# Latent attention's output divided by its sums between two 32 by 32 transpositions on VectorE, and the range test on ScalarE

## The chip, the cores and the metric

The kernel runs on one core of a Trainium2 chip. The core has five engines, each with a queue of its own: TensorE (PE in the profile; PEld is its loading of weights), VectorE (DVE), ScalarE (ACT), GpSimd (POOL) and SyncE (SP, which here only issues DMAs). TensorE writes its results to PSUM, which has eight banks of 512 float32 columns in 128 partitions. The metric is the time of one execution on the device in microseconds (us), the median of three runs.

## The reference

The input is x, 8 sequences of 1024 tokens with 256 features. Two blocks follow one another, each with a residual: x = x + attention(layernorm(x)), then x = x + local(layernorm(x)). The change concerns the first, a latent attention with 16 heads of 16 features and a rotary part of 32 that all heads share:

```python
c_kv = x @ W_kv_down
k_rope = _rotary_apply(c_kv @ W_k_rope, cos, sin)
k = (c_kv @ W_k_up).reshape(Bb, Tt, NH, HD)
v = (c_kv @ W_v_up).reshape(Bb, Tt, NH, HD)
q = (x @ W_q).reshape(Bb, Tt, NH, HD)
q_rope = _rotary_apply(x @ W_q_rope, cos, sin)
scores = jnp.einsum('bqhd,bkhd->bhqk', q, k)
scores = scores + jnp.einsum('bqr,bkr->bqk', q_rope, k_rope)[:, None]
scores = scores / scale
scores = jnp.where(causal[None, None], -jnp.inf, scores)
w = jax.nn.softmax(scores, axis=-1)
attn = jnp.einsum('bhqk,bkhd->bqhd', w, v).reshape(Bb, Tt, D_MODEL)
return attn @ W_o
```

The second block, two layers of windowed attention and a gated feed-forward part, takes the larger share of the time and isn't touched.

## The kernel before

The latent attention takes the eight sequences ("batches") one after the other, in 36 steps each. A step is one unit of scores: for one half c of the queries (512 columns), one group g of four heads and one block kb of 128 keys, TensorE computes four score blocks (sc, L422), transposed, with keys in the partitions. ScalarE takes their exponential (pt, L430). VectorE multiplies it by er (L444), the exponential of the shared rotary scores, which is computed once for all heads. TensorE then multiplies by the values (acc, L455). The values have a column of ones beside the 16 of each head, so acc holds, in 32 partitions for each head, 16 rows of output, one row of sums in row 16, and rows that nothing uses.

The work is staggered by steps. In step s TensorE's queue has the scores of unit s and then acc of unit s-2; VectorE's has the products of unit s-1. PSUM gives two pairs of banks to the scores, two banks to acc, and two banks in turn ("bank") to everything else. Everything else is put beside the steps by a table written by hand ("beside", with a step, a batch relative to the present one, a method and its arguments): the residual of the batch before, and the normalisation, projections and rotary scores of the next one or two. The methods are called in that order, and the order of the calls is the order of each engine's queue, for this part of the program. The local layers have an order of their own.

What the change touches:

- rotary (L395 to L406) computes one block of the shared rotary scores in a bank, psR. ScalarE writes er, the exponential, and with it the row sums (most). VectorE takes the row minima of er (least). GpSimd then cuts the triangle of the block on the diagonal. At the end of the stage most and least are compared with bounds (L609, L610): where exponentials are out of range, a flag makes a general version of the kernel run after this one.
- value (L369 to L382) computes the values of two token blocks, and VectorE copies them from PSUM (L76 in the helper).
- When acc of a group is complete, ScalarE copies it to SBUF (oaT). One step later, finished (L467 to L475) lets TensorE transpose it in four pieces of 128 by 128 (pst, L203), so that tokens lie in the partitions; VectorE takes the reciprocals of the sums (rs, L472) and multiplies (onat, L473).
- out_turn (L478 to L488) transposes two token blocks of onat back on TensorE (pso), and ScalarE copies them (oT). out_add (L490 to L501) multiplies by W_o (psx), VectorE adds x (L500), and a DMA stores the result.
- verdict (L1652 to L1657) tests rs for its range, three small VectorE instructions.
- In the last batch, out_turn and out_add of its first half are held back to the end ("held"), and only the attention itself is left after step 15.

Of the kernel before, what the change touches and what calls it, by code (L numbers as in the profile page):

```python
# [81 lines left out]
def preln_mla_local_kernel(  # L82
# [72 lines left out]
    def mla(ctx: ExitStack, verdict):  # L155
# [46 lines left out]
        def flip(out, t):  # L202
            nc.tensor.transpose(out, t, ident)  # L203
# [13 lines left out]
        nc.sync.dma_start(wknat, W_k_up)  # L217
        wv = wp.tile([P, D], F32, name="wv")
        nc.sync.dma_start(wv, W_v_up)
        wout = late.tile([P, 2, D], F32, name="wout")  # L220
        nc.sync.dma_start(wout, W_o.rearrange("(c p) d -> p c d", p=P))

# [42 lines left out]
        class Batch:  # L265
# [129 lines left out]
            def rotary(self, c, kb):  # L395
                q0, w, er = self.block(c, kb)
                ps = bank(f"psR{self.b}_{c}_{kb}")
                times(ps[:, :w], self.rk[:, kb * P : (kb + 1) * P], self.rq[:, q0 : q0 + w], True, True)
                n = 12 * self.b + 8 * (1 - c) + kb
                nc.scalar.activation(er, ps[:, :w], AF.Exp, scale=SCALE, accum_out=most[:, n : n + 1])  # L400
                nc.vector.tensor_reduce(least[:, n : n + 1], er, AX.X, ALU.min)  # L401
                if q0 == kb * P:
                    nc.gpsimd.affine_select(  # L403
                        out=er[:, :P], in_=er[:, :P], pattern=[[1, P]],
                        compare_op=ALU.is_ge, fill=0.0, base=0, channel_multiplier=-1,
                    )  # L406

            def start(self):
                b = self.b
                self.onat = late.tile([P, NT, NH, HD], F32, tag="onat", name=f"onat{b}")  # L410
                self.rs = small.tile([P, NT, NH], F32, tag="rs", name=f"rs{b}")
                self.acc = {}

            def scores(self, key, parts):

# [49 lines left out]
                return ended  # L465

            def finished(self, c, g, oT):  # L467
                ps = bank(f"pst{self.b}_{c}_{g}").rearrange("p (i h d) -> p i h d", i=4, h=4)
                for i in range(4):
                    flip(ps[:, i].rearrange("p h d -> p (h d)"), oT[:, i * P : (i + 1) * P])  # L470
                r = self.rs[:, 4 * c : 4 * c + 4, 4 * g : 4 * g + 4]
                nc.vector.reciprocal(r, ps[:, :, :, HD])  # L472
                nc.vector.tensor_tensor(  # L473
                    self.onat[:, 4 * c : 4 * c + 4, 4 * g : 4 * g + 4, :], ps[:, :, :, :HD],
                    r.unsqueeze(3).to_broadcast([P, 4, 4, HD]), ALU.mult,  # L475
                )

            def out_turn(self, t):  # L478
                if t == 4:
                    self.oTs, self.adds = {}, {}  # L480
                elif t == 0:
                    verdict(self.rs.rearrange("p t h -> p (t h)"), f"a{self.b}")
                ps = bank(f"pso{self.b}_{t}").rearrange("p (i q) -> p i q", i=4)
                for i in range(4):
                    flat = self.onat[:, t + i // 2].rearrange("p h d -> p (h d)")
                    flip(ps[:, i, :], flat[:, (i % 2) * P : (i % 2 + 1) * P])
                self.oTs[t] = late.tile([P, 4, P], F32, tag="oT", name=f"oT{self.b}_{t}", bufs=2)
                on_a(self.oTs[t], ps)  # L488

            def out_add(self, t, i, c=None):  # L490

                if i == 0 and not c:
                    self.adds[t] = bank(f"psx{self.b}_{t}").rearrange("p (i d) -> p i d", i=2)
                ps = self.adds[t]
                for n in range(2) if c is None else (c,):
                    times(ps[:, i], self.oTs[t][:, 2 * i + n, :], wout[:, n, :], n == 0, n == 1)
                if i == 1 and c != 0:
                    del self.oTs[t], self.adds[t]
                    two = slice(t, t + 2)
                    nc.vector.tensor_tensor(self.x[:, two, :], ps, self.x[:, two, :], ALU.add)  # L500
                    nc.sync.dma_start(x2d[self.b][:, two], self.x[:, two, :])  # L501
# [8 lines left out]
        for step, who, *what in (  # L510
            (0, -1, "out_add", 6, 1, 1), (0, 0, "query", 1, 1, 0),
            (1, 0, "query", 1, 1, 1),
            (2, 0, "value", 2),
            (3, 0, "keys", 1, 0), (3, 0, "keys", 1, 1, 0), (3, 1, "statistics", 1, 1),
            (4, 0, "keys", 1, 1, 1), (4, 0, "query", 0, 0, 0), (4, 1, "normalise", 0, 0),
            (5, 0, "query", 0, 0, 1), (5, -1, "out_turn", 0), (5, 1, "normalise", 0, 1),
            (6, -1, "out_add", 0, 0), (6, -1, "out_turn", 2), (6, 1, "normalise", 1, 0),
            (7, -1, "out_add", 0, 1), (7, -1, "out_add", 2, 0, 0),
            (8, -1, "out_add", 2, 0, 1), (8, -1, "out_add", 2, 1),
            (9, 0, "value", 3), (9, 0, "query", 1, 0, 0, 0),  # L520
            (10, 0, "query", 1, 0, 0, 1), (10, 0, "query", 1, 0, 1), (10, 1, "normalise", 1, 1),
            (11, 0, "rotary", 0, 0), (11, 1, "turn", 0, 0),
            (12, 0, "rotary", 0, 2), (12, 1, "down", 0, 0, 0), (12, 1, "turn", 0, 1),
            (13, 1, "down", 0, 0, 1), (13, 1, "down", 0, 1),
            (14, 0, "rotary", 0, 1),
            (15, 0, "rotary", 0, 3), (15, 1, "turn", 1, 0),
            (16, 1, "down", 1, 0), (16, 1, "turn", 1, 1),
            (17, 1, "down", 1, 1), (17, 1, "rope_q", 0, 0, 0),
            (18, 1, "rope_q", 0, 0, 1), (18, 1, "rope_q", 0, 1),
            (19, 1, "rope_q", 1, 0), (19, 1, "rope_k", 0, 0),  # L530
            (20, 1, "rope_k", 0, 1), (20, 1, "rope_q", 1, 1), (20, 2, "load"),
            (21, 1, "rope_k", 1), (21, 1, "query", 0, 1, 0, 0),
            (22, 1, "query", 0, 1, 0, 1), (22, 1, "query", 0, 1, 1),
            (23, 1, "keys", 0, 0), (23, 2, "statistics", 0, 0),
            (24, 1, "value", 0),
            (25, 1, "value", 1),
            (26, 1, "keys", 0, 1), (26, 2, "statistics", 0, 1),
            (27, 1, "rotary", 1, 0),
            (28, 1, "rotary", 1, 1),
            (29, 1, "rotary", 1, 2), (29, 1, "rotary", 1, 7),  # L540
            (30, 1, "rotary", 1, 3), (30, 0, "out_turn", 4),
            (31, 1, "rotary", 1, 6), (31, 0, "out_add", 4, 0),
            (32, 0, "out_add", 4, 1),
            (33, 1, "rotary", 1, 4),
            (34, 1, "rotary", 1, 5), (34, 0, "out_turn", 6), (34, 2, "statistics", 1, 0),
            (35, 0, "out_add", 6, 0), (35, 0, "out_add", 6, 1, 0),
        ):
            at(step, who, *what)
# [28 lines left out]
        line, done = [], []  # L577
        with tc.manual_schedule(engines={E.PE, E.DVE, E.Activation, E.Pool}):
            for b in range(B + 1):
                for step in range(len(units) if b < B else 9):  # L580
# [9 lines left out]
                        for bt, unit, pts in line[-2 : -1] if b < B else line[-1:] if step == 0 else []:  # L590
                            bt.turned(unit, pts)
                    if b == B and step == 0:
                        for act, args in held[:3]:
                            act(*args)
                    ended = []
                    if len(line) > 2 or b == B and line:
                        bt, unit, pts = line.pop(0)
                        ended = [(bt, e) for e in bt.values(unit, pts)]
                    if b == B and step == 0:
                        for act, args in held[3:]:  # L600
# [12 lines left out]

# [1139 lines left out]
```

## Time and profile before

| | us |
|---|---|
| median of three runs | 3512.26 (3509.98 to 3512.85) |
| the profiled execution, its own time | 3510.83 |
| its span, first to last instruction | 3509.0 |
| TensorE busy | 3449.8 |
| VectorE busy | 2439.9 |
| ScalarE busy | 1826.9 |
| GpSimd busy | 1350.3 |
| one middle batch of the latent attention (412.69 to 535.71) | 123.02 |

The granted TensorE clock is 0.997 of full speed. The latent attention takes from the start to about 1030 us, the local layers the rest. In the profile's lines an instruction is given by its line in the kernel, its engine, its operation, and what it writes and reads ("out<-in"). A helper's instructions all have the helper's line: L200 and L203 are TensorE's products and transpositions, L76 and L78 the copies from PSUM by VectorE and ScalarE. A group's line has the busy time and the mean length of one instruction, and after the second bar the idle time of the engine before these instructions, with what ended it. Instructions of one engine overlap a little[...], so that start to start is less than a length. A line of the table of waits has the total in us, the number of waits, and the longest.

### The profile page before, as it was taken

How to read it: one execution, taken by the hardware profiler on the slowest of the kernel's cores; microseconds unless marked ns; L12 is line 12 of the kernel's file. 1: busy time of each engine (PE TensorE's matmuls, PEld its weight loads, DVE VectorE, ACT ScalarE, POOL GpSimd, SP SyncE). 2: the span in 40 equal slices, each digit the busy share in tenths (PEclk: the TensorE clock that was granted, in tenths of full speed). 3: DMA queues.
4: the chain of work that ended last, by engine and by line, in shares of the span. 5: the costliest groups of instructions: out<-in, count | busy, mean ns of one | idle time of the engine just before them, and what ended most of it. 6: DMA issues, size and time to landing. Idle time of an engine off the chain costs nothing.

```text
span 3509.0 us, 81000 instructions
## 1 busy us (share of the span) xinstructions
PE 3449.8 (98%) x35714; PEld 1952.2 (56%) x35714; DVE 2439.9 (70%) x3529; ACT 1826.9 (52%) x2362; POOL 1350.3 (38%) x1031
## 2 busy tenths in 40 slices
PE   8999999999998999999999999999999999999999
PEld 2433443443345566666666666666666666666665
DVE  6888988988877766666675665666666566665654
ACT  5777777777653344444434444443444444444441
POOL 1000000100018555454554544555455454545540
PEclk9999999999999999999999999999999999999999
DMA  1000000000120010001011011111101110110011
GB/s 60 8 19 25 12 18 22 26 7 8 64 68 14 13 38 22 31 19 40 19 35 37 20 31 58 37 34 47 46 25 37 34 37 25 44 46 25 25 34 44
DMA packets 102966, 110.42 MB, mean 31 GB/s; under 512 B 12959, under 2 KB 87118, under 8 KB 102478
## 3 DMA queue, kind: packets, MB, share of 16 engines
q1 hardware_dynamic: 100622, 102.76, 9.3%
q8 instruction: 282, 4.62, 0.6%
q10 hardware_dynamic: 1984, 2.41, 0.2%
q14 instruction: 78, 0.64, 0.1%
HBM read 63.20 MB, written 41.94 MB: 30 GB/s over the span
## 4 chain that ended last, share of the span: by engine, by line
PE 91%; DVE 4%; ACT 2%; POOL 2%; issue 1%; DMA 1%; SPq 0%; ACTq 0%; DVEq 0%; POOLq 0%
PE ag L1007 16%; PE pair L819 12%; PE sc L422 9%; PE psy L1042 8%; PE acc L455 8%; PE psw L952 6%; PE o L919 6%; PE pv L846 6%; PE pair L879 3%; PE psq L860 3%; PE psR L200 2%; PE psx L200 2%; PE s L927 2%; PE psq L200 2%; DVE rs L931 1%; PE pst L203 1%
## 5 line engine op out<-in xcount | busy, mean ns | idle before, releaser
L444 DVE TENSOR_TENSOR pt<-pt,er 128x1024 f32<-128x1024 f32 x576 | 676.5, 1222 | 6.6 <-ACT pt L430 5.3
L430 ACT ACTIVATE pt<-sc 128x1024 f32<-128x1024 f32 x576 | 559.4, 1024 | 233.8 <-PE sc L422 210.6
L1007 PE MATMUL ag<-d,l 128*128 128x512 f32 x1408 | 641.0, 597 | 0.5 <-ACT d L763 0.4
L833 POOL TENSOR_TENSOR t<-t,t 128x1024 f32<-128x1024 f32 x128 | 301.3, 2354 | 765.2 <-DVE t L829 750.7
L819 PE MATMUL pair<-l_qkv,xT 128*128 128x512 f32 x1024 | 464.6, 596 | 3.7 <-ACT pt L884 1.8
L884 ACT ACT_TABLE_LOAD x120 | 154.0, 1283 | 543.4 <-PE pair L879 543.3
L1007 PEld LDWEIGHTS ag<-d,l 128*128 128x128 f32 x1408 | 262.0, 190 | 308.3 <-issue 303.7
L125 POOL TENSOR_TENSOR rn<-ss,half 128x16 f32<-128x16 f32 x128 | 375.8, 2936 | 13.5
L422 PE MATMUL sc<-q,k 32*128 32x512 f32 (+3 forms) x3072 | 346.5, 522 | 7.8 <-ACT pt L430 7.6
L931 DVE RECIPROCAL rs<-s 128x256 f32<-128x256 f32 x128 | 224.7, 1756 | 147.6 <-PE s L927 147.6
L826 DVE TENSOR_TENSOR t<-pair,l_cos 128x1024 f32<-128x1024 f32 x128 | 156.3, 1221 | 241.6 <-ACT sq L824 241.6
L819 PEld LDWEIGHTS pair<-l_qkv,xT 128*128 128x128 f32 x1024 | 188.7, 190 | 235.9 <-issue 203.9
L455 PE MATMUL acc<-pt,v 128*32 128x512 f32 (+3 forms) x3072 | 316.5, 497 | 0.1
L824 ACT ACTIVATE sq<-pair 128x1024 f32<-128x1024 f32 x128 | 131.1, 1024 | 298.6 <-issue 237.1
L1042 PE MATMUL psy<-l,hid 128*128 128x256 f32 x1280 | 281.5, 379 | 0.0
L1016 DVE SCALAR_TENSOR_TENSOR hid<-ag,l_b,ge 128x512 f32<-128x512 f32 x160 | 120.0, 750 | 225.0 <-ACT ge L1015 183.2
L1042 PEld LDWEIGHTS psy<-l,hid 128*128 128x128 f32 x1280 | 243.2, 190 | 46.7 <-issue 15.3
L884 ACT ACTIVATE pt<-pair 128x1024 f32<-128x1024 f32 (+1 forms) x256 | 234.8, 968 | 44.5 <-PE pair L879 43.2
L403 POOL TENSOR_SCALAR_AFFINE_SELECT er<-er 128x128 f32<-128x128 f32 x64 | 47.3, 740 | 529.1 <-DVE least L401 529.1
L839 POOL TENSOR_TENSOR t<-t,rn 128x1024 f32<-128x1024 f32 x128 | 243.6, 1903 | 10.0
L919 PEld LDWEIGHTS o<-pt,v 128*32 128x32 f32 x7680 | 201.9, 110 | 78.1 <-issue 70.1
L919 PE MATMUL o<-pt,v 128*32 128x128 f32 x7680 | 237.0, 275 | 5.0 <-POOL pt L886 5.0
(134 smaller groups left out, 5093.8 us busy)
## 6 DMA issues: line engine op xcount, KB each, us to landing
y<-xs SPq DMA_DIRECT2D x128, 128.0 KB
h<-y SPq DMA_DIRECT2D x32, 512.0 KB
x<-in_L_attn_x_dram SPq DMA_DIRECT2D x16, 512.0 KB
x2d<-x SPq DMA_DIRECT2D x32, 256.0 KB
xs<-x2d SPq DMA_DIRECT2D x16, 512.0 KB
x<-x2d SPq DMA_DIRECT2D x16, 512.0 KB
xs<-xs SPq DMA_DIRECT2D x32, 256.0 KB
xs<-xs SPq DMA_DIRECT2D x16, 512.0 KB
```

The costliest lines, as they stand in the source:

```text
L125: nc.gpsimd.tensor_tensor(out_, in_, half[:, :n], ALU.pow)
L422: nc.tensor.matmul(two[n // 2][:, n % 2, lo : lo + w], self.k[g][rows, kb * P : (kb + 1) * P], self.q[rows, g // 2, q0 : q0 + w], start=Tr ...
L430: nc.scalar.activation(pt, sc, AF.Exp, scale=SCALE)
L444: nc.vector.tensor_tensor(t, t, er.to_broadcast([P, 1024 // w, w]), ALU.mult)
L455: nc.tensor.matmul(self.acc[g][32 * n : 32 * n + 32, q0 - c * 512 :], self.v[:, kb, h * VW : h * VW + 32], pts[n // 2][:, n % 2, lo : lo + w],
L819: nc.tensor.matmul(qk[:, n].rearrange("p h d -> p (h d)"), self.left(i)[c], w["qkv"][:, c, n * INNER : (n + 1) * INNER], start=(c == 0), s ...
L833: nc.gpsimd.tensor_tensor(t1, t1, t2, ALU.add)
L884: nc.scalar.activation(pt[:, :, : n * P], flat[:, :, : n * P], AF.Exp, scale=-1.0)
L919: nc.tensor.matmul(o[32 * j : 32 * j + 32, g, a, :], vs[m][:, h * DH + a * 32 : h * DH + a * 32 + 32], pts[m][g][:, place(j), off : off + ...
L931: nc.vector.reciprocal(rs, s)
L1007: nc.tensor.matmul(ps, w["1"][:, c, i, :], d[:, c, :], start=(c == 0), stop=(c == 1))
L1042: nc.tensor.matmul(ps[:, t, :], hid[:, i, cols], w["2"][:, i, :], start=(t == i == 0), stop=False)
```

## The change

Six edits go together:

- finished: VectorE transposes oaT itself, in squares of 32 by 32 within each 32 partitions, all in one instruction of 128x512. A square belongs to one head and 32 tokens, so its row of sums becomes a column; the reciprocals have one number for each of 16 squares. The products of two groups (g even and odd) are put side by side in the two halves of the squares of one tile.
- turn_back, which is new, transposes that tile once more in the same way, a step after the second group is finished. The result, oT, has heads and features in the partitions again, in an order of its own.
- out_turn is gone, with its places in the table and in what is held back.
- out_add reads oT of the two pairs of groups. W_o is loaded with its rows in the order of oT, by eight DMAs of 16 partitions each and no longer by one.
- rotary: ScalarE takes a second exponential of the same scores, with the opposite sign, in place in PSUM, for its row sums; these stand for the minima in the range test. VectorE's minimum is gone.
- value: ScalarE copies the values in VectorE's place.

```diff
-        nc.sync.dma_start(wout, W_o.rearrange("(c p) d -> p c d", p=P))
+        for e in range(2):
+            for r in range(4):
+                lo = 32 * r + HD * e
+                nc.sync.dma_start(
+                    wout[lo : lo + HD],
+                    W_o.rearrange("(m e r p) d -> e r p m d", m=2, e=2, r=4)[e, r],
+                )
...
-                on_v(
+                on_a(
                     self.v[:, 2 * g : 2 * g + 2, : NH * VW].rearrange("p a (h d) -> p a h d", h=NH)[..., :HD],
...
                 nc.scalar.activation(er, ps[:, :w], AF.Exp, scale=SCALE, accum_out=most[:, n : n + 1])
-                nc.vector.tensor_reduce(least[:, n : n + 1], er, AX.X, ALU.min)
+                nc.scalar.activation(ps[:, :w], ps[:, :w], AF.Exp, scale=-SCALE, accum_out=least[:, n : n + 1])
...
             def finished(self, c, g, oT):
-                ps = bank(f"pst{self.b}_{c}_{g}").rearrange("p (i h d) -> p i h d", i=4, h=4)
-                for i in range(4):
-                    flip(ps[:, i].rearrange("p h d -> p (h d)"), oT[:, i * P : (i + 1) * P])
-                r = self.rs[:, 4 * c : 4 * c + 4, 4 * g : 4 * g + 4]
-                nc.vector.reciprocal(r, ps[:, :, :, HD])
+                nat = late.tile([P, 16, 32], F32, tag="onat", name=f"onat{self.b}_{c}_{g}", bufs=3)
+                nc.vector.transpose(nat.rearrange("p b d -> p (b d)"), oT)
+                r = self.rs[:, c, g]
+                nc.vector.reciprocal(r, nat[:, :, HD])
+                e = g % 2
+                if e == 0:
+                    self.onat[c, g // 2] = nat
                 nc.vector.tensor_tensor(
-                    self.onat[:, 4 * c : 4 * c + 4, 4 * g : 4 * g + 4, :], ps[:, :, :, :HD],
-                    r.unsqueeze(3).to_broadcast([P, 4, 4, HD]), ALU.mult,
+                    self.onat[c, g // 2][:, :, HD * e : HD * e + HD], nat[:, :, :HD],
+                    r.unsqueeze(2).to_broadcast([P, 16, HD]), ALU.mult,
                 )
-            def out_turn(self, t):
...
-                ps = bank(f"pso{self.b}_{t}").rearrange("p (i q) -> p i q", i=4)
-                for i in range(4):
-                    flat = self.onat[:, t + i // 2].rearrange("p h d -> p (h d)")
-                    flip(ps[:, i, :], flat[:, (i % 2) * P : (i % 2 + 1) * P])
-                self.oTs[t] = late.tile([P, 4, P], F32, tag="oT", name=f"oT{self.b}_{t}", bufs=2)
-                on_a(self.oTs[t], ps)
+            def turn_back(self, c, g):
+                if g % 2:
+                    t = late.tile([P, 512], F32, tag="oT", name=f"oT{self.b}_{c}_{g}", bufs=3)
+                    nc.vector.transpose(t, self.onat.pop((c, g // 2)).rearrange("p b d -> p (b d)"))
+                    self.oTs[c, g // 2] = t
+                if (c, g) == (0, 3):
+                    verdict(self.rs.rearrange("p c g b -> p (c g b)"), f"a{self.b}")
...
-                    times(ps[:, i], self.oTs[t][:, 2 * i + n, :], wout[:, n, :], n == 0, n == 1)
+                    col = (t + i) % 4 * P
+                    times(ps[:, i], self.oTs[t // 4, n][:, col : col + P], wout[:, n, :], n == 0, n == 1)
...
                     do(b, step)
+                    if turning:
+                        bt, e = turning.pop(0)
+                        bt.turn_back(*e)
                     if done:
                         bt, e = done.pop(0)
                         bt.finished(*e)
+                        turning.append((bt, e[:2]))
                     done += ended
...
-        nc.vector.tensor_scalar(ok[:, 1, :], least, 1 / TURN, None, ALU.is_ge)
+        nc.vector.tensor_scalar(ok[:, 1, :], least, TURN, None, ALU.is_le)
```

More of the change, by code (lines that the diff above doesn't have):

```diff
@@ L409, in start @@
                 b = self.b
-                self.onat = late.tile([P, NT, NH, HD], F32, tag="onat", name=f"onat{b}")
-                self.rs = small.tile([P, NT, NH], F32, tag="rs", name=f"rs{b}")
-                self.acc = {}
+                self.rs = small.tile([P, 2, 4, 16], F32, tag="rs", name=f"rs{b}")
+                self.acc, self.onat, self.oTs, self.adds = {}, {}, {}, {}
             def scores(self, key, parts):
@@ L467, in finished @@
             def finished(self, c, g, oT):
-                ps = bank(f"pst{self.b}_{c}_{g}").rearrange("p (i h d) -> p i h d", i=4, h=4)
-                for i in range(4):
-                    flip(ps[:, i].rearrange("p h d -> p (h d)"), oT[:, i * P : (i + 1) * P])
-                r = self.rs[:, 4 * c : 4 * c + 4, 4 * g : 4 * g + 4]
-                nc.vector.reciprocal(r, ps[:, :, :, HD])
+                nat = late.tile([P, 16, 32], F32, tag="onat", name=f"onat{self.b}_{c}_{g}", bufs=3)
[5 more added lines that the diff above has]
+                    self.onat[c, g // 2] = nat
                 nc.vector.tensor_tensor(
-                    self.onat[:, 4 * c : 4 * c + 4, 4 * g : 4 * g + 4, :], ps[:, :, :, :HD],
-                    r.unsqueeze(3).to_broadcast([P, 4, 4, HD]), ALU.mult,
-                )
-            def out_turn(self, t):
[L479 to L482, printed above, removed]
-                ps = bank(f"pso{self.b}_{t}").rearrange("p (i q) -> p i q", i=4)
-                for i in range(4):
-                    flat = self.onat[:, t + i // 2].rearrange("p h d -> p (h d)")
-                    flip(ps[:, i, :], flat[:, (i % 2) * P : (i % 2 + 1) * P])
-                self.oTs[t] = late.tile([P, 4, P], F32, tag="oT", name=f"oT{self.b}_{t}", bufs=2)
-                on_a(self.oTs[t], ps)
+                    self.onat[c, g // 2][:, :, HD * e : HD * e + HD], nat[:, :, :HD],
+                    r.unsqueeze(2).to_broadcast([P, 16, HD]), ALU.mult,
+                )
+            def turn_back(self, c, g):
[5 more added lines that the diff above has]
+                    verdict(self.rs.rearrange("p c g b -> p (c g b)"), f"a{self.b}")
             def out_add(self, t, i, c=None):
@@ L495, in out_add @@
                 for n in range(2) if c is None else (c,):
-                    times(ps[:, i], self.oTs[t][:, 2 * i + n, :], wout[:, n, :], n == 0, n == 1)
+                    col = (t + i) % 4 * P
+                    times(ps[:, i], self.oTs[t // 4, n][:, col : col + P], wout[:, n, :], n == 0, n == 1)
                 if i == 1 and c != 0:
-                    del self.oTs[t], self.adds[t]
+                    del self.adds[t]
                     two = slice(t, t + 2)
@@ L515, in mla @@
             (4, 0, "keys", 1, 1, 1), (4, 0, "query", 0, 0, 0), (4, 1, "normalise", 0, 0),
-            (5, 0, "query", 0, 0, 1), (5, -1, "out_turn", 0), (5, 1, "normalise", 0, 1),
-            (6, -1, "out_add", 0, 0), (6, -1, "out_turn", 2), (6, 1, "normalise", 1, 0),
+            (5, 0, "query", 0, 0, 1), (5, 1, "normalise", 0, 1),
+            (6, -1, "out_add", 0, 0), (6, 1, "normalise", 1, 0),
             (7, -1, "out_add", 0, 1), (7, -1, "out_add", 2, 0, 0),
@@ L540, in mla @@
             (29, 1, "rotary", 1, 2), (29, 1, "rotary", 1, 7),
-            (30, 1, "rotary", 1, 3), (30, 0, "out_turn", 4),
+            (30, 1, "rotary", 1, 3),
             (31, 1, "rotary", 1, 6), (31, 0, "out_add", 4, 0),
@@ L544, in mla @@
             (33, 1, "rotary", 1, 4),
-            (34, 1, "rotary", 1, 5), (34, 0, "out_turn", 6), (34, 2, "statistics", 1, 0),
+            (34, 1, "rotary", 1, 5), (34, 2, "statistics", 1, 0),
             (35, 0, "out_add", 6, 0), (35, 0, "out_add", 6, 1, 0),
@@ L576, in mla @@
         E = mybir.EngineType
-        line, done = [], []
+        line, done, turning = [], [], []
         with tc.manual_schedule(engines={E.PE, E.DVE, E.Activation, E.Pool}):
@@ L592, in mla @@
                     if b == B and step == 0:
-                        for act, args in held[:3]:
+                        for act, args in held[:2]:
                             act(*args)
@@ L599, in mla @@
                     if b == B and step == 0:
-                        for act, args in held[3:]:
+                        for act, args in held[2:]:
                             act(*args)
                     do(b, step)
+                    if turning:
+                        bt, e = turning.pop(0)
+                        bt.turn_back(*e)
                     if done:
```

## The prediction

> **What bounds the kernel now.** I read the page's busy line and chain first, then the busy time of one batch, then that batch's groups and waits, then the timeline around the instructions that change.
>
> From the page: busy time by engine, and the chain that ended last.
>
> ```profile
> PE 3449.8 (98%) x35714; PEld 1952.2 (56%) x35714; DVE 2439.9 (70%) x3529; ACT 1826.9 (52%) x2362; POOL 1350.3 (38%) x1031
> PE 91%; DVE 4%; ACT 2%; POOL 2%; issue 1%; DMA 1%; SPq 0%; ACTq 0%; DVEq 0%; POOLq 0%
> ```
>
> The change lies in the latent attention, which ends near 1030 us; TensorE's order in the local layers is the same in both programs. One batch of eight, from the table of stretches (length, then busy PE, PEld, DVE, ACT, POOL):
>
> ```profile
> 412.69:535.71 123.02, 122.01 (x1345) 49.37 (x1345) 108.24 (x141) 91.79 (x128) 9.72 (x10) 1.00 0.06 19
> ```
>
> TensorE fills 122.0 of 123.0 us and sets the pace; VectorE follows at 88%, ScalarE at 75%. What a transposition costs TensorE, from its timeline (start, length, idle before in brackets):
>
> ```profile
> 408.20 1.04 PE L200 MATMUL psq<-xnT,wq 128*32 128x512 f32 x8
> 409.18 1.14 PE L422 MATMUL sc<-q,k 32*128 32x512 f32 x8
> ...
> 411.13 1.04 PE L200 MATMUL psq<-xnT,wq 128*32 128x512 f32 x8
> 412.11 0.66 PE L203 MATMUL pst<-ident,oaT 128*128 128x128 f32 x4
> 412.69 1.14 PE L422 MATMUL sc<-q,k 32*128 32x512 f32 x8
> ...
> 450.45 0.66 PE L203 MATMUL psn<-ident,xn 128*128 128x128 f32 x4 [0.53 <-ACT er L400]
> ```
>
> From psq to sc is 0.98 us, and the pst between takes 0.58 more: a group of four costs 0.585 us of pace, not its 0.66 of length. The last line shows a second limit: a bank that ScalarE still reads stops TensorE for 0.53 us. VectorE's groups in one batch (busy, mean ns | idle before), and its only long waits:
>
> ```profile
> L444 DVE TENSOR_TENSOR pt<-pt,er 128x1024 f32<-128x1024 f32 x72 | 84.7, 1222 | 0.2
> L401 DVE TENSOR_REDUCE least<-er 128x1 f32<-128x512 f32 (+3 forms) x12 | 6.5, 549 | 6.8 <-ACT er L400 6.7
> L473 DVE TENSOR_TENSOR onat<-pst,rs 128x256 f32<-128x256 f32 x8 | 3.4, 424 | 0.3
> L76 DVE COPY v<-psv 128x512 f32<-128x512 f32 x4 | 2.8, 692 | 1.6 <-PE psv L200 1.5
> ...
> DVE rq L339 <- PE psrq L200: 2.4, 2, 2.3
> DVE x L500 <- PE psx L200: 1.6, 2, 0.8
> ```
>
> Of VectorE's 14.8 idle us, 6.7 are one thing: least stands in the queue and waits for er. Where VectorE is late, TensorE already feels it:
>
> ```profile
> 507.88 1.15 PE L422 MATMUL sc<-q,k 32*128 32x384 f32 x16
> 508.96 1.19 PE L455 MATMUL acc<-pt,v 128*32 128x256 f32 x14
> ...
> 509.98 0.39 PE L455 MATMUL acc<-pt,v 128*32 128x256 f32 x2
> ...
> 511.75 1.14 PE L422 MATMUL sc<-q,k 32*128 32x512 f32 x8
> ```
>
> This step takes 3.87 us, where one of the same make-up (532.19 to 535.71) takes 3.52: 0.35 us of waiting inside acc, after two steps in which VectorE had finished to do.
>
> **What the Trainium skill says.** "VectorE: DVE Perf Modes", The three transpose paths: VectorE transposes 32 by 32 blocks only, 311 ns for 128x128 in bf16; no run here shows it. "Vector Engine (DVE) Microarchitecture Reference", 3.8 The reshape front-end: the transposition sustains one element per cycle and lane. "ScalarE: Activation LUTs", What ACT_TABLE_LOAD costs: 186 ns plus 0.833 ns an element, neighbours overlapping by about 93 ns; the trace agrees (er of 512: 0.60 us against 613 ns; starts 0.47 apart where oaT precedes it). "TensorE: Matmul & The Clock Gate", Architectural detail: ScalarE and VectorE take their queues strictly in order; the wait of least above is just that.
>
> **The change, part by part.**
>
> 1. TensorE loses pst (64 groups of four) and pso (32): 96 x 0.585 = 56.2 us. Ten of them (six pst, four pso) lie after step 16 of the last batch, where VectorE sets the pace (it runs without a gap from 979 to 1018 us); they count in part 6. The other 86 are worth 50.3 us, 12 or 7.0 us in a full batch: 123.0 becomes 116.0.
>
> 2. VectorE, per batch. Gone: least 6.5 and v 2.8, with the idle time before them. Added: eight transpositions in finished, four in turn_back. The trace has none. 311 ns less 128 cycles at the 0.96 GHz in which the multiply's length fits (1024 elements, 1222 ns) leaves 178 ns; with 512 elements that is an estimate of 0.71 us by the skill. The nearest row, a copy of 128x512, has 0.69; starts lie 0.08 less apart (rq 472.08, next 472.68). I take 0.61 of pace; bounds 0.4, and 2.2 if four-byte elements take four cycles. 12 x 0.61 = 7.3. Reciprocal and multiply stay (0.28 and 0.34; from SBUF the same within 0.1). Sum: 108.2 - 9.3 + 7.3 = 106.2 of 116.0. VectorE isn't the bound, but has 92%.
>
> 3. Its lateness. I went through the steps with 2.33 us per pair of products, 1.23 for a finished, 0.61 for a turn_back. Up to step 31 VectorE keeps up. The residual add at step 32 must wait for the end of psx; behind it queue finished (32, 33), turn_back and statistics (34). The products for acc of steps 34, 35 and 0 then end 0.1, 0.8 and 0.4 us late, and in steps 3 to 6 (turn_back, the range check, statistics, normalise) 0.9 more. That is 2.2 us a batch against 0.35 before: +1.85 x 7 = 13 us. Bounds: 0 if I have the slack wrong by 1 us in favour, 25 if against. Who waits is acc, on TensorE.
>
> 4. ScalarE. Per batch 12 exponentials with their accumulator read: er is 0.50 of mean length, the read 0.21; by starts (36.90 to 37.48) 0.58 for 512 columns, about 0.5, 0.38 and 0.27 for the shorter: 5.9 us. v (4 copies) comes, oT (4 copies) goes: nothing. 91.8 + 5.9 = 98 of 116, so mostly hidden under TensorE; without that cover it would be 47 us. In place: behind the second exponential stand the next scores' exponentials. Step 29 has two (512 and 128 columns): ScalarE has 3.6 us against 3.2 of TensorE, and sc of step 31 comes 0.5 us late: +3.8 us over 7.5 batches.
>
> 5. Banks. psR stays taken until the second exponential ends: the wait of 0.53 in step 12 becomes 1.26, while pst's wait of 0.48 in step 15 goes with it: +0.25 x 7.5 = +1.9. The er blocks reach GpSimd's triangle masks earlier, since these waited for least; no cost.
>
> 6. The ends. Before 45 us nothing is overlapped: eight extra exponentials (4.2 us) and two v copies stand in ScalarE's queue, partly in its gaps: +3.5 (0 to 6). At the end VectorE takes four transpositions and three turns more, 4.4 us, against 3.7 us by which its last product (1018.0) led its acc (1021.7); then oaT, pst, pso and oT in series give way to oaT, two transpositions: about 1 us less. Net -0.5.
>
> 7. DMA. wout comes in eight loads on SP's queue, not one: some 8 x 0.4 us of issue, 2.8 more, ahead of batch 1's x. Its statistics (13.3 us) are followed by 6.9 us of idle VectorE before rq, which hides it; without cover 2.8 us. Two loads of xs (1 MB) move on SP's queue from before l_qkv to after the weights. ScalarE waits 6.9 us near 960 us for table loads that compete with them; at the 300 to 400 GB/s moved there 1 MB is about 3 us: I take -2 (-4 to +3).
>
> Sum: -50.3 + 13 + 3.8 + 1.9 + 3.5 - 0.5 - 2 = -30.6. The profiled execution took 3510.8 us (span 3509.0 and 1.8 around it), so 3480; the median shown, 3512.26, is 1.4 above: 3481.
>
> **The rivals.**
>
> - Hidden after all: parts 3 to 5 cost nothing. For it: least's 6.7 us of idle queue go. Against: VectorE at 92%. 3512 - 50.3 + 1.0 = 3463.
> - Transposition at half rate, pace 1.13: VectorE 112.5, its peak of lateness after step 34 grows by six times 0.53, 3.2 us a batch; the end 3.7. 3481 + 22 + 4 = 3507. For it: four-byte elements against the skill's two-byte row.
> - Slower: the transposition at four cycles an element, pace 2.2. Then VectorE has 98.9 + 12 x 2.2 = 125.3 and, with the 4.6 us of waits on rq, rk and x that remain, 130 a batch against 123: 7 x 7 + 3.5 + 7 x 1.6 at the end = +64, 3576. It decides from a pace of about 1.5 us (98.9 + 18 + 4.6 = 121.5, with the ends 123). For it only that no row shows the operation; against it the skill's one element per cycle.
> - The change does what it says only if the new test holds; a failed one would run the general version as well and double the time. Sums of exp of small scores are far below 1e17; I give it nothing.
>
> **How the numbers follow.** Forecast 0.57 (its own range 3466 to 3496), hidden 0.18, half rate 0.08, slower 0.14, else 0.03. The range 3452 to 3512 holds the first three and leaves out 0.14 and some of the rest. A measurement of this kernel tells about 0.2%, 7 us. Half of the half-rate case and a little more is same: 0.06; slower 0.16; faster 0.78.
>
> **What would show it.** A transposition of 128x512 at 0.6 to 0.75 us; a middle batch of 117 to 120 us with TensorE at 97% or more; VectorE 105 to 108 of it; waits of acc on pt near steps 34, 35, 4; psn waiting over 1 us for the second exponential. Wrong if a transposition takes over 1.2 us, if VectorE has no idle time in a batch, or if a batch is at 116.

## The result

The changed kernel takes 3501.74 us (median of nine runs, 3500.77 to 3502.12) where the kernel before took 3511.91 (nine runs beside it): a ratio of 0.9972, with a 95% interval from 0.9961 to 0.9982. It is 10 us faster, a third of the 30.6 us that was forecast. The span of the profiled execution went from 3509.0 to 3500.2 us.

From the page of the changed kernel, busy time by engine and the chain that ended last:

```profile
PE 3435.5 (98%) x35330; PEld 1931.8 (55%) x35330; DVE 2436.7 (70%) x3497; ACT 1867.6 (53%) x2554; POOL 1346.9 (38%) x1031
PE 90%; DVE 5%; ACT 2%; POOL 2%; DMA 1%; issue 0%; SPq 0%; ACTq 0%; POOLq 0%
```

TensorE has 384 instructions fewer, yet it is busy for only 14.3 us less, where 96 groups of 0.585 us were to go; the chain has one per cent more of VectorE. The same middle batch (length, then busy PE, PEld, DVE, ACT, POOL):

```profile
408.51:529.85 121.34, 120.34 (x1300) 47.25 (x1296) 107.73 (x139) 96.92 (x150) 9.51 (x10) 1.00 0.05 19
```

The batch is 1.7 us shorter, not 7. VectorE's groups in it:

```profile
L451 DVE TENSOR_TENSOR pt<-pt,er 128x1024 f32<-128x1024 f32 x73 | 85.6, 1219 | 7.6 <-ACT pt L437 7.6
L478 DVE STREAM_TRANSPOSE onat<-oaT 128x512 f32<-128x512 f32 x8 | 5.6, 704 | 0.0
...
L484 DVE TENSOR_TENSOR onat<-onat,rs 128x256 f32<-128x256 f32 x8 | 3.4, 425 | 0.3
...
L492 DVE STREAM_TRANSPOSE oT<-onat 128x512 f32<-128x512 f32 x4 | 2.8, 696 | 0.0
```

A transposition takes 0.70 us. VectorE no longer stands 6.7 us before least; it now stands 7.6 us before its products and waits for ScalarE, more than half of the 13.6 us in which it is idle. From the table of waits of the same batch, after:

```profile
PEld sc L429 <- ACT pt L437: 17.8, 29, 0.8
PEld acc L462 <- DVE pt L451: 11.3, 17, 0.8
...
PE psn L203 <- ACT psR L409: 1.0, 1, 1.0
```

And the first two before:

```profile
PEld sc L422 <- ACT pt L430: 12.0, 22, 0.8
...
PEld acc L455 <- DVE pt L444: 4.0, 6, 0.8
```

A weight load that waits is no loss by itself: these waits add up to 29 us, in a batch that lost 5.3. But TensorE stands more often at the limit of what ScalarE (scores) and VectorE (acc) have delivered. Where it does lose time can be read from the steps. I measure a step from the start of its scores to the start of the next one's, in the timelines. Twelve steps lost a group of transpositions. Five of them became shorter by what was forecast: 1, 6, 14, 27 and 32 by 0.59 us each. The others, and steps that lost none, gave 5.3 us of the 7.0 back:

| steps | against the length before less 0.585 for each group of transpositions, us | what lasts longer or shorter in them |
|---|---|---|
| 0, 5, 34 | +0.35, +0.98, +0.28 | acc |
| 35 | +0.92 | acc (0.57) and the scores (0.35) |
| 2, 7, 28, 33 | +0.22, +0.23, +0.54, +0.22 | the scores |
| 16, 29, 31 | +0.40, +0.52, +0.67 | the scores |
| 12 | +0.47 | psn's wait for its bank |
| 15 | -0.12 | the scores by +0.44, a wait for a bank by -0.55 |
| 30 | -0.34 | acc, which had waited before |

How such a loss looks, from the timeline of the changed kernel in steps 27 and 28 (start, length):

```profile
495.06 0.59 ACT L78 COPY oaT<-acc 128x512 f32<-128x512 f32 x1
...
495.53 1.29 ACT L372 ACTIVATE k<-psk,mask 128x512 f32<-128x512 f32 x2
...
496.68 1.97 ACT L437 ACTIVATE pt<-sc 128x1024 f32<-128x1024 f32 x2
...
498.15 1.68 PE L429 MATMUL sc<-q,k 32*128 32x256 f32 x16
...
498.70 0.73 PEld L429 LDWEIGHTS sc<-q,k 32*128 32x128 f32 x12 [0.25 <-ACT pt L437]
```

The same 16 score products in the kernel before:

```profile
501.18 1.15 PE L422 MATMUL sc<-q,k 32*128 32x256 f32 x16
```

In the changed kernel the later ones wait inside the group for the pair of banks that the second half of pt (until 498.65) still reads; pt began late because oaT and two key copies stand ahead of it on ScalarE. They stood there before, too; but then TensorE had a transposition of 0.585 us to do in the meantime. Note that the 0.53 us of waiting count as busy time of PE. In this kernel TensorE's busy share is no sign of how much of it is work.

### The profile page after: what moved, and what is told of

Its sections match the earlier page's. It is cut to its first block, busy times and chain, and to the rows that moved or that the text cites. A ratio compares the mean times of both kernels' runs of the same rounds, so it can differ in the third digit from the quotient of the medians.

```text
span 3500.2 us, 80321 instructions
## 1 busy us (share of the span) xinstructions
PE 3435.5 (98%) x35330; PEld 1931.8 (55%) x35330; DVE 2436.7 (70%) x3497; ACT 1867.6 (53%) x2554; POOL 1346.9 (38%) x1031
## 4 chain that ended last, share of the span: by engine, by line
PE 90%; DVE 5%; ACT 2%; POOL 2%; DMA 1%; issue 0%; SPq 0%; ACTq 0%; POOLq 0%
PE ag L1019 16%; PE pair L831 12%; PE sc L429 9%; PE psy L1054 8%; PE acc L462 8%; PE psw L964 6%; PE o L931 6%; PE pv L858 6%; PE pair L891 3%; PE psq L872 3%; PE psq L200 2%; PE s L939 2%; PE psx L200 2%; PE psR L200 1%; DVE rs L943 1%; DVE pt L451 1%
## 5 line engine op out<-in xcount | busy, mean ns | idle before, releaser
L429 PE MATMUL sc<-q,k 32*128 32x512 f32 (+3 forms) x3072 | 369.9, 522 | 5.0 <-ACT pt L437 4.9
L462 PE MATMUL acc<-pt,v 128*32 128x512 f32 (+3 forms) x3072 | 333.2, 496 | 3.5 <-DVE pt L451 3.1
L429 PEld LDWEIGHTS sc<-q,k 32*128 32x128 f32 x3072 | 157.3, 184 | 199.8 <-ACT pt L437 154.4
```

Of the source, the lines that this page charges most:

```text
L429: nc.tensor.matmul(two[n // 2][:, n % 2, lo : lo + w], self.k[g][rows, kb * P : (kb + 1) * P], self.q[rows, g // 2, q0 : q0 + w], start=Tr ...
L462: nc.tensor.matmul(self.acc[g][32 * n : 32 * n + 32, q0 - c * 512 :], self.v[:, kb, h * VW : h * VW + 32], pts[n // 2][:, n % 2, lo : lo + w],
```

## The experiments

All times are medians, with the kernel before, run beside them, at 3511.1 to 3511.8 us. "A batch" is a middle one, 123.0 us before and 121.3 after. When I wrote the first expectations I held that both engines had given the gain back, ScalarE some 2.5 us of a batch and VectorE 3.2 ("both"); the rivals were one of them alone.

**The two halves of the change, each alone.** In the changed kernel, the minima and the value copies back on VectorE; in the kernel before, only these moved to ScalarE, with the transpositions left on TensorE.

```diff
-                nc.scalar.activation(ps[:, :w], ps[:, :w], AF.Exp, scale=-SCALE, accum_out=least[:, n : n + 1])
+                nc.vector.tensor_reduce(least[:, n : n + 1], er, AX.X, ALU.min)
...
-                on_a(
+                on_v(
```

> The transpositions alone on VectorE: the changed kernel with the minimum and the copies of the values back on VectorE, so ScalarE has no extra work but loses oT. VectorE then needs 107.7 + 9.3 = 117.0 us a batch and has the waits for er of the kernel before in its queue (6.7 us). 'Both': VectorE becomes the bound, 123.5 to 125 a batch, 3515 to 3527. Rival 'TensorE': its 7.0 us of removed transpositions count as long as VectorE stays below TensorE's pace, as without the second exponential: 119.5 a batch, 3487.

> ScalarE's part alone: the kernel before with the second exponential and the copies of the values on ScalarE, transpositions on TensorE as before. 'Both': TensorE's transpositions give ScalarE time in steps 14, 27, 28 and 30, so only the bank in step 12 (0.5) and perhaps step 31 come to wait, and the wait of 0.35 in step 30 goes: 123.0 to 123.5 a batch, 3513 to 3518 with the start. Rival 'the exponentials cost the same wherever': the 1.9 us a batch that leaving them out gave are lost here too: 124.9, 3529.

Transpositions alone: 3533.84 us, a ratio of 1.0062 (1.0048 to 1.0075), slower than before; a batch takes 125.7 us.

```profile
419.70:545.38 125.68, 123.29 (x1300) 47.73 (x1296) 115.66 (x155) 89.93 (x122) 7.96 (x10) 1.00 0.06 18
```

VectorE now has 115.7 us to do in its queue's order, and in 5.7 us more its minima wait for er. So acc lasts longer in steps 0, 4, 5, 16, 17, 29 to 31, 34 and 35: VectorE's lateness eats the 7.0 us of TensorE and 2.7 more, a little beyond what "both" had said (125). ScalarE's half alone: 3516.57 us, 1.0016 (1.001 to 1.0023), 0.6 us a batch. The wait in step 12 is there in full (+0.48), and steps 15 and 32 grow by 0.27 and 0.12. But in steps 29 to 31, where the next run will show 1.0 us, nothing is lost (-0.04, -0.32, +0.07). The -0.32 isn't the exponentials' doing: with the minima gone from VectorE's queue, the wait of acc that step 30 had before is gone. So "the exponentials cost the same wherever" falls: with the transpositions still on TensorE they cost 0.6 us, or 0.9 without that gain, and in the changed kernel, as the next run shows, 1.9. Each half alone makes the kernel slower (by 23 and 5 us), the two together make it 10 us faster.

**No second exponential.** The lower half of the range test is left out.

```diff
-                nc.scalar.activation(ps[:, :w], ps[:, :w], AF.Exp, scale=-SCALE, accum_out=least[:, n : n + 1])
```

> The changed kernel without ScalarE's second exponential; the lower half of the range test is left out (its sums are set to 1). Theory 'both': of the 5.3 us per batch that came back, about 2.5 stem from ScalarE (steps 12, 16, 28, 29, 31) and 3.2 from VectorE (steps 33 to 7); so a middle batch falls from 121.3 to about 118.9 and the start by 2: 3481. Rival 'VectorE': late products set the pace and take over at once when ScalarE is relieved: a batch stays above 120.8, 3497. Rival 'ScalarE': VectorE is late only because exponentials are; both cure: 116.3 a batch, 3461.

3487.16 us, 0.993 (0.9916 to 0.9943); a batch 119.45 us, 1.9 less than in the changed kernel, between "both" (118.9) and "VectorE" (120.8). Four steps become shorter, 12, 16, 29 and 31, by 0.48, 0.40, 0.56 and 0.46. In step 12 it is the bank that comes free earlier; in the other three the scores' exponentials no longer stand behind a second exponential. Step 28, which "both" had counted in, stays as it was, as do 2 and 33. The mechanism of steps 29 and 31, from the timeline of the changed kernel:

```profile
499.53 0.66 ACT L409 ACTIVATE psR<-psR 128x512 f32<-128x512 f32 x1
...
500.13 2.00 ACT L437 ACTIVATE pt<-sc 128x1024 f32<-128x1024 f32 x2
...
501.62 1.71 PE L429 MATMUL sc<-q,k 32*128 32x384 f32 x16
```

and the same scores without the second exponential:

```profile
493.34 1.15 PE L429 MATMUL sc<-q,k 32*128 32x384 f32 x16
```

**VectorE's order.** Two edits that change no work, only its place. First, the statistics and normalisations of the next batches are moved from steps 34 and 3 to 6 to quieter steps (the pair of 34 and 3 to 30 and 31, the four normalisations to 9, 10, 11 and 12). Second, turn_back and finished are issued ahead of what the table puts beside a step:

```diff
-                    do(b, step)
                     if turning:
...
                         turning.append((bt, e[:2]))
+                    do(b, step)
```

> The changed kernel with VectorE's statistics moved from steps 34 and 3 to steps 30 and 31, and its normalisations from steps 4, 5, 6, 10 to 9, 10, 11, 12, where VectorE waits. 'Both': VectorE's part of the waits, 3.2 us, falls to about 1: 119.2 a batch, 3484. 'VectorE': the same or more. 'ScalarE': no change, 3500.

> The changed kernel with turn_back and finished issued ahead of the step's side work, so that they don't stand behind the residual add, which waits 2.0 us for psx in step 32. Theory 'order': the wait of 0.93 in step 35 goes, and those in 33 and 34 shrink: 120.3 a batch, 3493. Rival: the products of these steps are late because their exponentials are; no change, 3501.

> Both changes of VectorE's order together: finished ahead of the side work, and statistics and normalisations moved to steps in which VectorE waits. If the two waits are separate: 120.04 - 0.93 = 119.1 a batch, 3486. If one takes the other's place: 119.8 or more, 3491.

Moved: 3493.90 us, 0.995 (0.9936 to 0.9963). First: 3493.17 us, 0.9948 (0.9935 to 0.9962). Both: 3489.13 us, 0.9936 (0.9923 to 0.995), a batch of 119.44 us, again 1.9 less. The first came out at 120.0 us a batch where 119.2 were expected, the second at 120.05 for 120.3, the third at 119.44 for 119.1. The two together give 1.9 us and not the sum of 2.6, since each of them cures the wait at step 0 and part of the one at step 5. Step 5 of the changed kernel shows what is cured:

```profile
418.06 0.75 DVE L291 BATCH_NORM_STATS2 bnst<-x 128x6 f32<-128x256 f32 x2
...
419.14 0.70 DVE L492 STREAM_TRANSPOSE oT<-onat 128x512 f32<-128x512 f32 x1
...
420.31 0.29 DVE L1661 TENSOR_REDUCE good<-oka 128x1 f32<-128x128 f32 x1
...
420.51 2.35 DVE L451 TENSOR_TENSOR pt<-pt,er 128x1024 f32<-128x1024 f32 x2
...
421.92 1.62 PE L462 MATMUL acc<-pt,v 128*32 128x512 f32 x6
...
423.37 0.60 PE L462 MATMUL acc<-pt,v 128*32 128x512 f32 x2
```

Statistics, turn_back and the range check together hold the products back until 420.51, the second of them ends at 422.86, and acc, which needs 1.06 us, lasts from 421.92 to 423.97. With both edits VectorE is a step ahead and acc runs through:

```profile
413.56 5.75 DVE L451 TENSOR_TENSOR pt<-pt,er 128x1024 f32<-128x1024 f32 x5
...
416.62 1.06 PE L462 MATMUL acc<-pt,v 128*32 128x512 f32 x8
```

At steps 32 to 35 the reason is the one that the prediction named. In the changed kernel the residual add waits 2.0 us for psx with finished behind it; with finished first the transposition fills that wait. After:

```profile
515.37 0.69 DVE L508 TENSOR_TENSOR x<-psx,x 128x512 f32<-128x512 f32 x1 [2.00 <-PE psx L200]
...
515.98 0.70 DVE L478 STREAM_TRANSPOSE onat<-oaT 128x512 f32<-128x512 f32 x1
...
517.35 2.35 DVE L451 TENSOR_TENSOR pt<-pt,er 128x1024 f32<-128x1024 f32 x2
```

With both edits:

```profile
507.36 0.70 DVE L478 STREAM_TRANSPOSE onat<-oaT 128x512 f32<-128x512 f32 x1
...
509.09 0.69 DVE L508 TENSOR_TENSOR x<-psx,x 128x512 f32<-128x512 f32 x1 [0.28 <-PE psx L200]
509.70 2.35 DVE L451 TENSOR_TENSOR pt<-pt,er 128x1024 f32<-128x1024 f32 x2
```

That is 0.28 us saved at step 34 and 0.30 at step 35.

**No transposition back.** turn_back hands on the tile that isn't transposed (onat with six buffers), so the output isn't the reference's; VectorE has 2.8 us a batch less to do.

> The changed kernel without the second transposition: out_add reads the tile that wasn't turned back, so the attention's output is not the right one. VectorE loses 2.8 us a batch, of which 0.6 each at steps 34 and 3 matter: 'both' 120.1 a batch and 1.8 less at the end, 3490; 'ScalarE' no change but for the end, 3500.

3494.33 us, 0.995 (0.9936 to 0.9963); a batch 120.2 us, 1.13 less, all of it at steps 0 and 5 (0.35 and 0.81). These 2.8 us of VectorE are worth 1.1, no more than moving the statistics is (1.3).

**Second exponentials of the later queries behind the next scores' exponentials.** The edit keeps them out of the way of pt, in exchange for a bank that stays taken for longer.

> The changed kernel with the second exponentials of the upper half's blocks (steps 27 to 34) issued behind the scores' exponentials of the next step, none left out. 'Both': the waits of the scores at steps 28, 29 and 31, 1.7 us, go, if no bank is then missed: 119.6 a batch, 3489. 'VectorE': no change, 3501. If the bank is the limit, psR waits for it in steps 29 and 30 instead and nothing is gained.

3522.75 us, 1.0031 (1.0019 to 1.0042); a batch 124.3 us. Steps 29, 30 and 31 take 4.13, 4.77 and 4.76 us, 3.0 more in all: TensorE waits for the bank. The expectation had named the bank as what could spoil it, but not that it would cost this much. The second exponential stands between two limits: ahead of pt it delays the scores, behind the next scores it holds the bank.

**Part of the work given to the other engine.** To the kernel with finished first and the statistics moved, three runs add: the minima of the first 512 columns on VectorE again (steps 11 to 15); one of ScalarE's key copies on VectorE (this one added to the changed kernel); and all together.

```diff
+                if c:
                     nc.scalar.activation(ps[:, :w], ps[:, :w], AF.Exp, scale=-SCALE, ...)
+                else:
+                    nc.vector.tensor_reduce(lowest[...], er, AX.X, ALU.min)
...
+                    if (m, n, e) == (0, 1, 1):
+                        nc.vector.tensor_scalar(self.k[1][:, HALF[1]], ps, mask[:, 1:2], None, ALU.mult)
+                        continue
```

> The kernel with finished first and the statistics moved, and of the second exponentials only those of the later 512 columns (eight a batch) left on ScalarE: for the first 512 columns (four a batch, steps 11 to 15) VectorE takes the minimum of er again. Theory 'held banks': the waits of steps 12 and 16 (0.48 and 0.40 us) come from a bank that the second exponential holds, so both go: a batch of 118.6 us instead of 119.4, 3482 us. Rival 'the queue': the minimum waits on VectorE for er, as it did in the kernel before, and the products behind it come late: a batch stays at 119.4 or above, 3489 us or more.

> The changed kernel, with one of ScalarE's key copies (the second of step 26) on VectorE. Theory 'uncovered': step 28 takes 3.47 us, although it lost a transposition of 0.585 us, since oaT and two key copies stand ahead of an exponential on ScalarE, which the transposition had hidden. With one copy (0.69 us) gone step 28 falls to about 2.95 us, a batch to 120.8, the time to 3498 us. Rival 'VectorE' : the copy makes the products as late as the exponential was, and nothing is gained: 121.3 us a batch, 3502 us.

> All of it together: finished first, statistics moved, minima of the first 512 columns on VectorE, one key copy on VectorE. If the causes add up: a batch of 118.1 us, 3478 us. If VectorE, at some 111 of 118 us, becomes the bound, no better than without the key copy and the minima: 3489 us.

Minima: 3488.25 us, 0.9934 (0.992 to 0.9947). A batch takes 118.96 us, between the two expectations. Steps 12 and 16 fall by 0.48 and 0.40, and in step 17 acc, late, gives 0.38 back, as the rival said. Only step 12 is a held bank; at step 16 it is the scores that had waited. The gain of the whole to the run without this edit, 0.9 us, is less than the intervals can tell. Key copy: 3506.37 us, 0.9985 (0.9979 to 0.9992), worse than the changed kernel; a batch 122.1 us. This is a miss; the timeline of its steps 26 to 28 tells why:

```profile
497.75 0.75 DVE L373 TENSOR_SCALAR k<-psk,mask 128x512 f32<-128x512 f32 x1 [2.66 <-ACT k L375]
...
499.49 2.35 DVE L454 TENSOR_TENSOR pt<-pt,er 128x1024 f32<-128x1024 f32 x2
...
500.81 1.71 PE L465 MATMUL acc<-pt,v 128*32 128x512 f32 x6
```

In VectorE's queue the copy stands ahead of statistics and products, and it waits 2.66 us, with them behind it: the queues are taken strictly in order, as the Trainium skill has it ("TensorE: Matmul & The Clock Gate", Architectural detail), and this trace agrees. So acc comes late, step 28 grows from 3.47 to 4.12 us, 29 and 30 by 0.15 and 0.49, against 0.51 gained at 31. All three together: 3500.49 us, 0.9969 (0.9957 to 0.9981), worse than both expectations, with 109.9 us of VectorE in a batch of 121.0. That left open what step 28 would do with ScalarE's queue shorter and VectorE's unchanged.

**The same key copy left out.** No engine does it; the scores of group 1 take group 0's keys in its place.

> The changed kernel with one of ScalarE's key copies (the second of step 26) left out altogether: the scores of head group 1 take the keys of group 0 in the second half, so the output isn't the reference's. VectorE gets nothing more to do. Theory 'uncovered': step 28 falls from 3.47 us to about 2.95, since that exponential stands behind one copy less, a batch to 120.8, the time to 3498 us. Rival 'VectorE': step 28 is as long as before, because the products of the step are late and not the exponential; 121.3 us a batch, 3502 us.

3498.55 us, 0.9961 (0.9948 to 0.9975), a batch of 120.92 us. Step 28 falls from 3.47 to 3.04, and nothing else changes. From its timeline, the lines that answer to those of the changed kernel above:

```profile
493.51 0.59 ACT L78 COPY oaT<-acc 128x512 f32<-128x512 f32 x1
...
493.98 0.71 ACT L374 ACTIVATE k<-psk,mask 128x512 f32<-128x512 f32 x1
494.73 1.94 ACT L440 ACTIVATE pt<-sc 128x1024 f32<-128x1024 f32 x2
...
496.60 1.26 PE L431 MATMUL sc<-q,k 32*128 32x256 f32 x16
```

One copy less ahead of pt, and the scores take 1.26 us instead of 1.68. So "uncovered" holds for step 28: ScalarE's queue, with work that the change hadn't touched, cost 0.43 of the 0.54 us there.

**Do the causes add up?** Finished first, statistics moved and no second exponential; and the same with the key copy left out.

> Finished first and the statistics moved, and no second exponential (the lower half of the range test is left out). If the causes add up: 119.44 less 1.88 = 117.6 us a batch, 3475 us. If the exponentials and VectorE's order hide behind one another, as much as 118.5 and 3482 us.

> The last kernel with the key copy of step 26 left out too (neither the lower half of the range test nor the reference's output). Theory 'uncovered': 0.5 us a batch less than it, 117.1 us, 3471 us. Rival: VectorE, nothing gained, 117.6 us.

3475.38 us, 0.9896 (0.9881 to 0.9912), and 3474.41 us, 0.9895 (0.9879 to 0.991). The first:

```profile
395.48:512.85 117.37, 116.84 (x1300) 45.72 (x1296) 107.63 (x138) 91.86 (x127) 10.30 (x10) 1.00 0.06 19
```

Expected was 117.6 us from the sum; 117.4 were measured, so these two causes hide nothing from each other (together they give 0.18 us more at step 35 than apart). The key copy's 0.42 at step 28 is still there to be had, but in this kernel it comes back at once, at steps 29 (+0.11) and 35 (+0.29), where scores and acc wait next: "uncovered" gives 0.4 us alone and nothing here. Beside the 120.34 us of the changed kernel, TensorE is busy for 116.84 with the same products: 3.5 us of that busy time had been waiting.

**What is left.** No run took away the waits of the scores at steps 2, 7, 15 and 33 (moving the statistics only shifts the one at 7 to 6), nor the rest of those at 28, 31 and 35. They can be read from the traces. Steps 1 and 2 of the changed kernel:

```profile
408.05 1.14 PE L429 MATMUL sc<-q,k 32*128 32x512 f32 x8
...
409.23 1.94 ACT L437 ACTIVATE pt<-sc 128x1024 f32<-128x1024 f32 x2 [1.29 <-PE sc L429]
...
410.98 1.36 PE L429 MATMUL sc<-q,k 32*128 32x512 f32 x8
```

Here ScalarE isn't late because of other work: it stood idle for 1.29 us and waited for these very scores. But the scores of a step fill both pairs of banks, and the two exponentials that empty them end 3.12 us after the step began. With the transposition gone, step 1 lasts 2.93 us, and the later scores of step 2 wait until the second pair is read. The same happens wherever a step gets shorter than that, in each of these kernels:

| step, in which kernel | its length | what the scores of the next step take longer |
|---|---|---|
| 1, 6 and 32, changed | 2.93 | 0.22 to 0.23 |
| 14, changed | 2.72 | 0.44 |
| 5, finished first and statistics moved | 2.92 | 0.23 |
| 34, the same without the second exponential | 2.73 | 0.43 |
| 30, no second exponential | 2.95 | 0.21 |
| 27, key copy left out | 3.04 | 0.11 |

The two columns add up to about 3.15 us each time. The kernel before has it too, in a step that never had a transposition (2.93 us long, and scores of 1.38 us where 1.15 are normal):

```profile
485.37 1.15 PE L422 MATMUL sc<-q,k 32*128 32x256 f32 x16
...
488.30 1.38 PE L422 MATMUL sc<-q,k 32*128 32x384 f32 x16
```

In the changed kernel that is 1.1 us after steps 1, 6, 14 and 32, and some 0.5 more behind the other waits at 28, 31 and 35. It is an account from the traces of several kernels; no run changed the banks or the length of these exponentials alone.

## Why the prediction was wrong

The direction held, and so did most of what was priced; the gain came out at a third, because of terms that weren't. By the forecast's own parts, for a middle batch in us:

| part | forecast | measured | what shows it |
|---|---|---|---|
| 1, TensorE's transpositions | -7.0 | -7.0 | TensorE does without them; five steps show the full 0.59 |
| 1, scores that then wait for the exponentials of a step under 3.15 us | 0 | +1.6 | the traces, not a run of its own |
| 3, VectorE late | +1.85 | +1.8 | acc in steps 0, 5, 34 and 35, less the 0.34 of before; finished first and statistics moved |
| 4, second exponentials ahead of the scores' exponentials | +0.5 | +1.6 | the runs without them (16, 29, 31; 0.2 at 35) |
| 4, a key copy ahead of them, uncovered | 0 | +0.4 | the key copy left out |
| 5, banks, steps 12 and 15 | +0.25 | -0.1 | the run without second exponentials; the lengths of step 15 |
| length of a batch | 118.6 | 121.3 | |

- Two steps failed. The larger is in part 1: "12 or 7.0 us in a full batch: 123.0 becomes 116.0" sets nothing against the removed time, as if no step had another limit than TensorE. Where a step fell to 2.93 or 2.72 us, the next one's scores waited for the exponentials, which end 3.12 us after a step's start even where ScalarE was idle before them: 1.6 us a batch.
- The smaller is in part 4: "91.8 + 5.9 = 98 of 116, so mostly hidden under TensorE". The busy time was about right (96.9), but it was set against a whole batch. In steps 27 to 31 ScalarE has no slack, and the cover had been the transpositions themselves. The wait named for step 31 came (0.46 for 0.5), those of steps 16 and 29 were missed; with the key copy it is 2.0 us for 0.5.
- Part 2 was right: the Trainium skill's row in "VectorE: DVE Perf Modes", The three transpose paths, had given an estimate of 0.71 us for a transposition, and 0.70 was measured; VectorE's 106.2 us became 107.7. The half-rate and the slower rival fall with it.
- Part 3 had the size and the cause (the residual add that waits for psx with finished behind it), and the places but for details: 34, 35, 0 and 5. Curing it gave 1.9 us, although acc gained 2.2: some came back as scores that wait at step 35.
- Part 5 had the right bank in step 12 (the forecast wait 1.26, measured 1.00) and the gain in step 15 (0.48 forecast, 0.55 in the step's length). What came back at step 15, 0.44, is a wait of the scores.
- The batch is 2.7 us longer than forecast; over 7.5 batches that would be the 20 us that are missing. That it fits so well is in part luck, since the rest was off both ways. Part 6: VectorE's first product came 2.07 us later (3.5 forecast), and from its last product to the local layers it took 1.0 us less (0.5 forecast). Part 7: the first batch is 0.39 us longer than before where the middle ones are 1.7 shorter, and the local layers take 1.0 us more, not 2 less. Whether the eight loads of W_o and the order of xs do that wasn't tried.
- Of what was to show it, the transposition (0.70), VectorE's 107.7 us, the waits of acc near steps 34 and 35, and psn's wait (1.0) were as stated; the middle batch, at 117 to 120, was not. "Hidden after all" falls with it. The fastest kernels here, at 3474 and 3475 us, leave out the second exponential and so half of the range test.

A version that computes all that both kernels do, with finished first and the statistics moved, takes 3489.13 us, 0.6% less than before.

## What to carry to other kernels

When work is taken off the bounding engine, ask at each place what the other engines did during it: the removed time was their slack. It can be gone in two ways. Either another engine is busy just there, with what is queued ahead of it; so price an added instruction not against the mean busy share of a stage but in the step where it stands, after the removal. Or another engine is idle, but the chain through it (here scores, exponentials, free banks) is as long as the step; so add up that chain, and take it as the pace that the steps can't stay below. And look at how long the same group of products lasts beside its shortest; the busy share of TensorE stays at 98 to 99% while it waits inside its groups.

## What the runs showed of the hardware

- VectorE transposes 128x512 float32 in 32 by 32 squares in 0.70 us, as long as it takes to add two tiles of that size (0.69).
- An exponential of 128x512 with its row sums takes ScalarE 0.622 us in place in PSUM, and 0.624 from PSUM to SBUF; reading the accumulator adds an instruction of 0.22 us, but only about 0.1 us between two starts (508.77 to 509.35 for the pair of 0.61 and 0.22, where a copy of that size goes 0.47 to its neighbour).
